# Two-layer graph attention: the third outer Strassen product by block products, a second set of sums, one order for all groups

## The chip, the cores and the metric

One core of a Trainium2 chip runs the whole kernel. The metric is the device time of one execution in microseconds, the median of several runs. TensorE (PE) multiplies and writes to PSUM banks; VectorE (DVE) and ScalarE (ACT) read and write PSUM and SBUF; GpSimd (POOL) works on SBUF; DMA transfers are issued by SyncE (SP), a few by ACT and POOL.

## The reference

128 graphs with 128 nodes and 512 features go through two attention layers with 8 heads of 64.

```
# layer 0
Q, K, V = x @ W_q + b_q, x @ W_k + b_k, x @ W_v + b_v          # by heads
scores  = Q K^T / 8 + (x @ w_g[:D])[:, None] + (x @ w_g[D:])[None, :] + b_g + log(adj + 1e-9)
x       = softmax(scores) @ V + x
# layer 1
q, k, v = x @ Wq.T + bq, x @ Wk.T + bk, x @ Wv.T + bv
logits  = q k^T / 8 + log(clip(adj, 1e-8))
out     = (softmax(logits) @ v) @ Wo.T + bo
x       = layer_norm(x + out) * gamma + beta
```

All of it is float32.

## The kernel before

**Groups.** Four graphs make a group. 32 groups (t = 0 to 31) are layer 0, the next 32 (t = 32 to 63) layer 1. A group of layer 0 has three matrices (v, q, k), each a 512 x 512 product for 4 x 128 rows; from t = 33 on each group also does the output matrix o of the group before it. Then come the scores of two graphs at a time (8 matmuls a graph, so 32 profile records for two graphs), an exponential on ACT, a product with the adjacency on DVE, and mixing with V (`mix`, 16 matmuls a graph), whose result DVE divides by the sums and writes to a tile `o`.

**Outer Strassen.** A matrix is a two-by-two product of 256 x 256 quarters with seven products P1 to P7 instead of eight. The sums of x that they need (T1 to T4, tiles `T`) are made by POOL in `outer_sums`, the sums of the weights once per weight in `combine_outer`. A product done plainly (`product`) is four units; a unit is two matmuls of 64 rows of output and 256 columns each (the two "halves", which run side by side). It takes one bank of PSUM. Each matmul is two records in the profile.

**Inner Strassen.** The products in `Strassen.INSIDE` are themselves split in 128 x 128 blocks with seven leaves (`inner`); a leaf is two half matmuls of 128 columns. Their sums come from POOL: `inner_sums` (tiles `innerB`, `innerT`) and, for weights, `combine_inner` (tile `wi`). One such product has this run in its bank: ACT fills two blocks with zero; stage 1 is two leaves; ACT copies one block to `s5` and another within the bank; stage 2 is two leaves; DVE adds `s5` to a block; stage 3 is two leaves; DVE adds again; stage 4 is one leaf. Every stage waits for the engine before it, so PE does other products, scores or mixing in between.

**A matrix.** `matrix` uses three banks: A0 or A1 by turns for P1, P6, P7 and P4, bank C for P2, bank B for P5 and, accumulated on it, P3. ACT or DVE copy partial results out (`t1`, `u2`, `u3`), and DVE adds a bank to one of these to make a quarter of the result. The first group of each layer (t = 0, 32) does all products plainly while POOL prepares the weights' inner sums. So 217 matrices of 223 have inner products: 62 groups of three, and 31 output matrices.

**Order.** Nothing is issued as it is written down. `Plan` records each operation with a cost and its predecessors, `schedule` makes list schedules with several margins, takes the best, and `refine` moves operations where PE would wait. `issue` then issues all engines' instructions in that order. Each engine runs its own in order. Every instruction therefore has one line in the profile, that of `issue` (L498); tile names tell them apart. TensorE's units have a position (`PLAIN`, `INNER_AT`, `PERIOD`) that gives a first order.

**Buffers.** `T` has one set for all groups; `innerB` and `innerT` have two each; `o` has two. The natural x of even groups of layer 0 lies in weight slot 3 (`spare`), whose weight is needed only in layer 1. In layer 1 `store_blocks` sends `o` to DRAM in four transfers for two graphs, and `load_mixed` reads it back turned.

Of the kernel before, what the change touches and what calls it, by code (L numbers as in the profile page):

```python
# [13 lines left out]
ALU = mybir.AluOpType  # L14
# [3 lines left out]
H, P, G, S = 8, 128, 4, 32  # L18
# [25 lines left out]
class Strassen:  # L44
# [6 lines left out]
    }  # L51
    SUMS = {"T1": ("B12", "B11"), "T2": ("B22", "T1"), "T3": ("B22", "B12"), "T4": ("T2", "B21")}
    RAW = {(0, 0): A11, (1, 0): A12, (1, 1): NA22, (0, 1): S3}
    INSIDE = ("P1", "P2", "P4", "P5")

    @staticmethod
    def load(engines, t, w):
# [39 lines left out]
        }  # L97


class Plan:  # L100


# [22 lines left out]

    def __init__(self, tc):
        self.tc, self.nc = tc, tc.nc
        self.ops, self.seen, self.masks, self.open, self.log = [], {}, {}, None, []
        for name in self.ENGINES:
            setattr(self, name, Plan.Engine(self, name))  # L130

    @contextmanager
    def unit(self, pos, cost):
# [25 lines left out]
    @staticmethod  # L159
    def cost(engine, method, aps, kw, args):  # L160
        n = max(a.free_size() if callable(a.free_size) else a.free_size for a in aps)
        psum = any(a.space == PSUM for a in aps)
        if method == "dma_start":
            if engine == "gpsimd":
                return 2.3, 6.5
            kb = (aps[0].size() if callable(aps[0].size) else aps[0].size) * 4 / 1024
            return 0.68 if len(aps[0].shape) == 4 else 0.47, 1.8 + kb / 150
        if engine == "scalar":
            return (0.06 + 0.00085 * n + (0.08 if "scale" in kw or "bias" in kw else 0.0) + (0.13 if "accum_out" in kw else 0.0),)
        if engine == "vector":  # L170
            if method in ("transpose", "bn_stats"):
                return (0.01 + 0.00118 * n,)
            if not psum and method in ("tensor_tensor", "tensor_scalar_mul") and n == 512:
                return (1.2,)
            return (0.08 + 0.00103 * n + (0.055 if method == "scalar_tensor_tensor" else 0.0),)
        if ALU.pow in args:
            return (0.68,)
        return (0.135 + 0.00216 * n,)
# [97 lines left out]
    def edges(self, margin, late=0.0):  # L276
        after, before = ([[] for _ in self.ops] for _ in range(2))
        for o in self.ops:
            for p in o.preds:
                wait = self.wait(self.ops[p], o) + margin * (o.engine == "tensor") + late * (self.ops[p].lag or self.CALM * (o.engine == "sync"))  # L280
                after[p].append((o.i, wait))
                before[o.i].append((p, wait))
        return after, before
# [54 lines left out]
    def refine(self, seq, before, lates):  # L338
# [123 lines left out]
        self.log.append(("refined", gained))  # L462
        return seq

    def schedule(self):
        ops, best, draw = self.ops, None, Random(1)
        _, judged = self.edges(self.JUDGED)
        lates = [
            [(0.7 * (draw.random() < 0.15), draw.expovariate(1.0) * self.ROUGH) if o.lag else (0.0, 0.0) for o in ops]
            for _ in range(self.TRIALS)  # L470
        ]
        for margin in self.MARGINS:
            after, before = self.edges(margin, self.LATE)
            key = self.first_keys(after, before)
            for n in range(self.PASSES):
                start = self.run(after, key)
                turn = sorted(ops, key=lambda o: (start[o.i], o.i))
                end = sum(self.retime(turn, judged, late) for late in lates) / self.TRIALS
                self.log.append(round(end, 1))
                if best is None or end < best[0]:  # L480
                    best = end, turn, start
                back = self.run(before, [-start[o.i] - o.cost for o in ops])
                key = [-back[o.i] - o.cost for o in ops]
                if n >= self.PASSES // 2:
                    key = [k + draw.uniform(0.0, self.STIR) for k in key]
        turn = [o.i for o in best[1]]
        for _ in range(self.SWEEPS):
            turn = self.refine(turn, judged, lates)
            self.log.append(round(sum(self.retime([ops[i] for i in turn], judged, late) for late in lates) / self.TRIALS, 1))
        self.turn = [ops[i] for i in turn]  # L490
        for o in ops:
            o.start, o.ls = best[2][o.i], 0.0
        return self.turn

    def issue(self):
# [5 lines left out]
def fast_path(ctx, tc, args, GOOD, bad):  # L501
# [8 lines left out]
    D2 = D // 2  # L510
    Q = P // S
    SCALE = 1.0 / HD**0.5
    LEAF = 0.2167
    HALVES = slice(0, P // 2), slice(P // 2, P)
    assert N == P and HD == 64 and KC == 4 and G == 4 and NG * G == B

# [31 lines left out]
    XNB = place("xn", 2, D, count=2)  # L548
    spare = W_[3][0].rearrange("p q k e -> p q (k e)")
    TB = place("T14", 2, 2, 2, N), place("T23", 2, 2, 2, N)  # L550
    TOB = [v.rearrange("p i (g c n) -> p i g c n", g=2, n=N) for v in XNB]
    INNER_B, INNER_T = Ring(place("innerB", 2, 4, N, count=2)), Ring(place("innerT", 2, 3, N, count=2))
    GW = place("gw", KC, D)
    VB = place("v", 2, 2, H, HD + 1, count=2)
    QT, KT = place("qT", 2, 4 * N, count=2), place("kT", 2, 4 * N, count=2)
    T1, U2, U3 = Ring(place("t1", 4 * N, count=2)), place("u2", 4 * N), place("u3", 4 * N)
    S5 = Ring(place("s5", N, count=4))
    HSB, OR = place("h", 2, D, count=2), Ring(place("o", 2, D, count=2))
    ROW, GAMMA, BETA, BV = place("row", D), place("gamma", D), place("beta", D), place("bv", KC)
    ZERO, ones, ident = place("zero", 2, N), place("ones", P // 2), place("ident", P)  # L560
    BQ, BK = place("bq", KC, count=2), place("bk", KC, count=2)
    bg, minus_half, good_sum, eps = place("bg", 1), place("minus_half", G), place("good_sum", 1), place("eps", 1)
    CB, GATEB, GATED = place("c", 2, G, count=2), place("gate", G, count=2), Ring(place("gated", H, count=2))
# [9 lines left out]
    def split(t):  # L573
        return t // NG, t % NG
# [57 lines left out]
    def inner_sums(xt, Bs, T):  # L632


        xs = xt[:, 0:2].rearrange("p g (k c) n -> p g k c n", k=2)
        for y, (b11, b12, b21, b22), names in (
            (INNER_B.take(), (xs[:, 0, :, 0], xs[:, 1, :, 0], xs[:, 0, :, 1], xs[:, 1, :, 1]), ("P1", "P2")),
            (INNER_T.take(), (T[:, :, 0, 0], T[:, :, 1, 0], T[:, :, 0, 1], T[:, :, 1, 1]), ("P5", "P4")),
        ):
            t1, t2, t4 = (y[:, :, j] for j in range(3))  # L640
            t3 = y[:, :, 3] if names[0] == "P1" else b12
            nc.gpsimd.tensor_tensor(t1, b12, b11, ALU.subtract)
            nc.gpsimd.tensor_tensor(t2, b22, t1, ALU.subtract)
            nc.gpsimd.tensor_tensor(t3, b22, b12, ALU.subtract)
            nc.gpsimd.tensor_tensor(t4, t2, b21, ALU.subtract)
            for k, i in enumerate(names):
                Bs[i, "inner"] = {
                    j: q[:, k] for j, q in dict(P1=b11, P2=b21, P3=b22, P4=t4, P5=t1, P6=t2, P7=t3).items()
                }


# [35 lines left out]
    def inner(i, W, Bs, bank, side, pos):  # L687
# [10 lines left out]
                    l, r = (a[j], b[j]) if side == "w" else (b[j], a[j])  # L698
                    matmul(blocks[:, at], l, r, False, True)

        nc.scalar.copy(blocks[:, C21 : 4 : 3 - C21], ZERO)
        leaves(pos[0], ("P5", 3), ("P1", C21))
        nc.scalar.copy(s5, blocks[:, 3])
        nc.scalar.copy(blocks[:, 0], blocks[:, C21])
# [4 lines left out]
        leaves(pos[3], ("P4", C21))  # L709

    PLAIN = dict(P1=10, P6=22, P7=36, P4=62, P5=38, P3=55, P2=30)
    INNER_AT = dict(P1=(0, 6, 11, 16), P4=(54, 59, 64, 69), P5=(26, 31, 43, 48), P2=(28, 33, 45, 50))
    PERIOD = 64 - 3 * len(Strassen.INSIDE)

    def matrix(n, W, Bs, side, dst, bias=None, row=None, inside=Strassen.INSIDE):
# [34 lines left out]
        add(0, 0, c, t1)  # L750
        make("P7", a, False)
        copy(u3, a, 1)
        make("P5", b, True)
        add(1, 1, b, u3)
        make("P3", b, False)
        add(0, 1, b, u2)
        make("P4", a, True)
        add(1, 0, a, u3)
# [51 lines left out]
    def score(t, graphs, pos):  # L810


        slots = [SLOTS.take() for _ in graphs]
        with nc.unit(pos, 0.92 * len(graphs) + 0.2):
            for s, b in zip(slots, graphs):
                for c in range(KC):
                    for r in range(2):
# [113 lines left out]

    tc.nc.vector.memset(ones, 1.0)
    make_identity(tc.nc, ident)
    nc.gpsimd.memset(ZERO, 0.0)
    nc.gpsimd.memset(GOOD, 0.0)
    nc.gpsimd.memset(minus_half, -0.5)
    nc.gpsimd.memset(eps, LN_EPS)
# [24 lines left out]
    n = 0  # L962
    waiting = None
    for t in range(LAST):
        L, g = split(t)
        if t == NG:
            weights(WQ, 1, 0, w_q1t)
            Strassen.combine_outer(nc.gpsimd, WQ[1][0])
            weights(WK, 1, 1, w_k1t)
            Strassen.combine_outer(nc.gpsimd, WK[1][0])  # L970
            weights(WV, 1, 3, w_v1t)
            Strassen.combine_outer(nc.gpsimd, WV[1][0])
            weights(WO, 1, 2, w_o1t)
            nc.sync.dma_start(ROW, b_o1.partition_broadcast(P))
            for c in range(KC):
                weigh_rows(c)
            Strassen.combine_outer(nc.gpsimd, WO[1][0])
# [11 lines left out]
            Strassen.combine_outer(nc.vector, WQ[0][0])  # L989
            Strassen.combine_outer(nc.vector, WK[0][0])  # L990
        TS[t] = quarters(XT[t])
        outer_sums(TS[t], TB)
        plain = t in (0, NG)
        if not plain:
            inner_sums(XT[t], TS[t], TB[0])
        if L == 0:
            gates(t)
        for which in "qkv" if t == NG else "vqk":
            if which == "v" and t != NG and t > NG + 1:
                end_attention(*waiting)  # L1000
                waiting = None
            elif which == "q" and waiting is not None:
# [13 lines left out]
        if t > NG:  # L1016
# [7 lines left out]
            if t < LAST - 1:  # L1024
                norm_and_store(u)

    t, u, a = LAST - 1, LAST - 2, n
    place_ = {"at": 0}

# [82 lines left out]
    nc.vector.tensor_scalar(bad, good, 4 * B * H * P - 0.5, None, ALU.is_lt)  # L1112
    begin_one(t, 3, HL[:, 3])
    finish_one(t, 3, HL[:, 3])
    nc.issue()


# [190 lines left out]
```

## Time and profile before

| | |
|---|---|
| median of 3 runs | 3164.75 us (3164.16 to 3164.99) |
| profiled execution, its own time | 3164.5 us |
| its span, first to last instruction | 3162.7 us |
| granted TensorE clock, mean | 0.997 |
| busy PE, PE weight loads | 3116.2, 2597.6 us |
| busy DVE, ACT, POOL | 2057.8, 1605.6, 2063.4 us |

A row of a group view reads: line, engine, operation, output<-inputs, shapes, count | busy us, mean ns of one | idle time of the engine before them, and what ended it. A row of the stretches reads: stretch, its length, then busy time with the number of instructions of PE, PE weight loads, DVE, ACT and POOL, then the granted clock, the share of the DMA engines and GB/s. A row of the instructions in order of time reads: start, length, what, how many. Matmuls are pipelined, so the length of one is longer than the step from one start to the next.

### The profile page before, as it was taken

How to read it: one execution, taken by the hardware profiler on the slowest of the kernel's cores; microseconds unless marked ns; L12 is line 12 of the kernel's file. 1: busy time of each engine (PE TensorE's matmuls, PEld its weight loads, DVE VectorE, ACT ScalarE, POOL GpSimd, SP SyncE). 2: the span in 40 equal slices, each digit the busy share in tenths (PEclk: the TensorE clock that was granted, in tenths of full speed). 3: DMA queues.
4: the chain of work that ended last, by engine and by line, in shares of the span. 5: the costliest groups of instructions: out<-in, count | busy, mean ns of one | idle time of the engine just before them, and what ended most of it. 6: DMA issues, size and time to landing. Idle time of an engine off the chain costs nothing.

```text
span 3162.7 us, 114044 instructions
## 1 busy us (share of the span) xinstructions
PE 3116.2 (99%) x47790; PEld 2597.6 (82%) x47790; DVE 2057.8 (65%) x4424; ACT 1605.6 (51%) x4528; POOL 2063.4 (65%) x2307
## 2 busy tenths in 40 slices
PE   9999999999999999999999999999999999999997
PEld 6888888888888888878888888888888888888885
DVE  5666666666666666656666666666666666666666
ACT  3555555555555545544545454544545454544543
POOL 8656666665666656696766757576766757575764
PEclk9999999999999999999999999999999999999998
DMA  5555455555555555544344443535353443535353
GB/s 128 122 119 119 103 109 123 112 109 122 110 115 105 112 120 109 127 122 102 76 111 98 104 110 90 123 85 121 85 122 84 103 110 92 122 86 121 85 110 90
DMA packets 963062, 341.43 MB, mean 108 GB/s; under 512 B 864240, under 2 KB 871408, under 8 KB 962544
## 3 DMA queue, kind: packets, MB, share of 16 engines
q1 hardware_dynamic: 944272, 299.48, 41.1%
q0 software_dynamic: 16864, 32.51, 5.9%
q8 instruction: 378, 6.19, 0.8%
q10 hardware_dynamic: 1408, 2.10, 0.2%
q14 instruction: 140, 1.15, 0.1%
HBM read 192.42 MB, written 141.56 MB: 106 GB/s over the span
## 4 chain that ended last, share of the span: by engine, by line
PE 91%; POOL 3%; ACT 2%; DVE 1%; issue 1%; DMA 0%; SPq 0%; DVEq 0%; POOLq 0%; ACTq 0%
PE bankA L498 44%; PE bankB L498 22%; PE s L498 15%; PE bankC L498 10%; ACT u L498 1%; POOL w L498 1%; POOL wi L498 1%; ACT h L498 0%; POOL T L498 0%; POOL innerB L498 0%; SPq L498 0%; DVE xT L498 0%; POOL rs L498 0%; POOL h L498 0%; POOL xn L498 0%
## 5 line engine op out<-in xcount | busy, mean ns | idle before, releaser
L498 PE MATMUL bankA<-T,w 128*64 128x256 f32 (+1 forms) x5648 | 757.4, 353 | 7.3 <-ACT u L498 5.7
L498 PEld LDWEIGHTS bankA<-T,w 128*64 128x64 f32 x5648 | 366.6, 137 | 95.5 <-ACT u L498 14.2
L498 DVE TENSOR_TENSOR bankA<-bankA,s 128x128 f32<-128x128 f32 x868 | 255.1, 294 | 282.3 <-PE bankA L498 229.9
L498 PE MATMUL bankA<-w,T 128*64 128x256 f32 (+1 forms) x2824 | 385.5, 352 | 2.4 <-POOL T L498 2.3
L498 PE MATMUL bankB<-xT,w 128*64 128x256 f32 x2048 | 306.6, 380 | 0.1
L498 ACT COPY bankB<-zero 128x256 f32<-128x256 f32 x217 | 81.6, 376 | 422.5 <-DVE kT L498 169.6
L498 DVE TENSOR_TENSOR bankB<-bankB,s 128x128 f32<-128x128 f32 x434 | 127.9, 295 | 210.4 <-PE bankB L498 183.5
L498 PEld LDWEIGHTS s<-qT,kT 64*128 64x128 f32 x4096 | 238.6, 188 | 30.0 <-issue 22.0
L498 PE MATMUL s<-qT,kT 64*128 64x128 f32 x4096 | 263.1, 278 | 0.1
L498 ACT COPY bankA<-zero 128x256 f32<-128x256 f32 x434 | 164.4, 379 | 192.1 <-DVE u L498 108.0
L498 POOL TENSOR_TENSOR xn<-gw 128x512 f32<-128x512 f32 x62 | 79.1, 1276 | 258.7 <-DVE gw L498 81.5
L498 POOL TENSOR_TENSOR T<-xT 128x512 f32<-128x512 f32 x128 | 162.2, 1287 | 118.5 <-PE bankB L498 59.6
L498 ACT COPY s<-bankA 128x128 f32<-128x128 f32 x434 | 116.5, 268 | 232.1 <-PE bankA L498 225.8
L498 PEld LDWEIGHTS bankA<-w,T 128*64 128x64 f32 x2824 | 182.4, 137 | 36.0 <-POOL T L498 4.1
L498 DVE SCALAR_TENSOR_TENSOR h<-adjT,s 128x1024 f32<-128x1024 f32 x128 | 154.7, 1215 | 68.9 <-ACT s L498 68.3
L498 ACT ACTIVATE gw<-gw 128x512 f32<-128x512 f32 x256 | 163.0, 640 | 52.6 <-POOL gw L498 51.1
L498 POOL TENSOR_TENSOR gw<-w,gw 128x512 f32<-128x512 f32 x128 | 161.9, 1286 | 41.4 <-ACT gw L498 41.4
L498 POOL TENSOR_TENSOR gw<-xn,gw 128x512 f32<-128x512 f32 x128 | 161.6, 1283 | 37.2 <-ACT gw L498 37.1
L498 DVE TENSOR_TENSOR bankC<-bankC,s 128x128 f32<-128x128 f32 x434 | 126.7, 292 | 90.4 <-PE bankC L498 66.0
L498 PE MATMUL bankA<-w,xn 128*64 128x256 f32 x1364 | 183.6, 352 | 0.0
L498 DVE STREAM_TRANSPOSE xT<-xT 128x512 f32<-128x512 f32 x252 | 172.9, 695 | 12.4 <-DMA xT<-in_x_dram 10.4
L498 DVE SCALAR_TENSOR_TENSOR xT<-adjT,s 128x1024 f32<-128x1024 f32 x124 | 148.8, 1215 | 46.4 <-ACT s L498 41.5
(218 smaller groups left out, 8827.0 us busy)
## 6 DMA issues: line engine op xcount, KB each, us to landing
xT<-x1d_b SPq DMA_DIRECT2D x64, 512.0 KB, 6.4
xT<-in_x_dram SPq DMA_DIRECT2D x496, 64.0 KB, 2.9
x1d_o<-o SPq DMA_DIRECT2D x248, 128.0 KB, 4.5
gw<-x1d_o SPq DMA_DIRECT2D x62, 512.0 KB, 3.5
h<-x1d_n POOLq DMA_DIRECT2D x62, 512.0 KB, 9.7
out_dram<-h SPq DMA_DIRECT2D x60, 512.0 KB, 2.9
xn<-in_x_dram SPq DMA_DIRECT2D x32, 512.0 KB, 4.5
x1d_n<-w SPq DMA_DIRECT2D x32, 512.0 KB, 3.0
```

Of the source, the lines that this page charges most:

```text
L498: self.tc.keep_in_program_order(getattr(getattr(self.nc, engine), method)(*args, **kw))
```

## The change

P3 becomes an inner product: it gets its own turn in bank B or C by turns, and DVE adds that bank to `u2` before `u2` is added to P5's bank. POOL makes three more block sums (`inner3`, two buffers) and one in place; the `innerB` sum that had a fourth column is now also made in place. `wi` has room for five products, and `combine_inner` makes the sums of five. The zero fill no longer copies a tile of zeros: ACT multiplies the identity matrix, read twice, by zero. `o` has one buffer. Even groups of layer 0 put their outer sums into idle parts of slot 3 (`TB0`). In layer 1 the v weights are loaded and combined first, and group 32 does v, q, k like the others. `schedule` orders the operations of groups 1 to 31 and of 34 to 62 by one written list of keys per layer (`PATTERNS`), repeated for each group, before `refine` runs; some of the planner's costs are changed.

```diff
-    INSIDE = ("P1", "P2", "P4", "P5")
+    INSIDE = ("P1", "P2", "P3", "P4", "P5")
...
+PATTERNS = (
+    (1, 31, 42.01, [int(v) for v in '''
+        413 877 68 1327 2833 345 136 0 481 1462 1395 1039 549 2070 3356 809 626 694 1573 2772 8615 4503 9355 9402
...
+    (34, 62, 52.97, [int(v) for v in '''
...
+    def periodic(self, start):
+
+        ops, marks, key, shift = self.ops, self.marks, list(start), 0.0
+        for first, last, period, at in self.patterns:
...
+            for t in range(first, last + 1):
+                for r, x in enumerate(at):
+                    key[marks[t] + r] = origin + period * (t - first) + x / 100
...
+        heap, seq = [], []
+        for o in ops:
+            if not left[o.i]:
+                heappush(heap, (key[o.i], o.i))
+        while heap:
+            i = heappop(heap)[1]
+            seq.append(i)
+            for j in after[i]:
+                left[j] -= 1
+                if not left[j]:
+                    heappush(heap, (key[j], j))
+        return seq
...
-        turn = [o.i for o in best[1]]
+        turn = self.periodic(best[2])
...
+    TB0 = [
+        v.rearrange("p (i g c) n -> p i g c n", i=2, g=2)
+        for v in (W_[3][0][:, 4:6].rearrange("p q k (c n) -> p (q k c) n", n=N), W_[3][1].rearrange("p i j n -> p (i j) n")[:, 0:8])
+    ]
...
-    INNER_B, INNER_T = Ring(place("innerB", 2, 4, N, count=2)), Ring(place("innerT", 2, 3, N, count=2))
+    INNER_B, INNER_T, INNER_3 = (
+        Ring(place(name, n, 3, N, count=2)) for name, n in (("innerB", 2), ("innerT", 2), ("inner3", 1))
+    )
...
-    HSB, OR = place("h", 2, D, count=2), Ring(place("o", 2, D, count=2))
+    HSB, OR = place("h", 2, D, count=2), Ring(place("o", 2, D, count=1))
...
+            (INNER_3.take(), (ys[:, 0, 1:, 0], ys[:, 1, 1:, 0], ys[:, 0, 1:, 1], ys[:, 1, 1:, 1]), ("P3",)),
         ):
             t1, t2, t4 = (y[:, :, j] for j in range(3))
-            t3 = y[:, :, 3] if names[0] == "P1" else b12
             nc.gpsimd.tensor_tensor(t1, b12, b11, ALU.subtract)
             nc.gpsimd.tensor_tensor(t2, b22, t1, ALU.subtract)
-            nc.gpsimd.tensor_tensor(t3, b22, b12, ALU.subtract)
+            nc.gpsimd.tensor_tensor(b12, b22, b12, ALU.subtract)
             nc.gpsimd.tensor_tensor(t4, t2, b21, ALU.subtract)
...
-        nc.scalar.copy(blocks[:, C21 : 4 : 3 - C21], ZERO)
+        nc.scalar.mul(blocks[:, C21 : 4 : 3 - C21], ident.rearrange("p (o n) -> p o n", o=1).to_broadcast([P, 2, N]), 0.0)
...
-    INNER_AT = dict(P1=(0, 6, 11, 16), P4=(54, 59, 64, 69), P5=(26, 31, 43, 48), P2=(28, 33, 45, 50))
+    INNER_AT = dict(P1=(0, 6, 11, 16), P3=(9, 14, 19, 24), P4=(54, 59, 64, 69), P5=(30, 35, 43, 48), P2=(3, 8, 13, 18))
...
+        if "P3" in inside:
+            d = (b, c)[n % 2]
+            make("P3", d, True)
+            nc.vector.tensor_tensor(u2, d, u2, ALU.add)
         make("P5", b, True)
         add(1, 1, b, u3)
-        make("P3", b, False)
+        if "P3" not in inside:
+            make("P3", b, False)
         add(0, 1, b, u2)
...
         if t == NG:
+            weights(WV, 1, 3, w_v1t)
+            Strassen.combine_outer(nc.gpsimd, WV[1][0])
             weights(WQ, 1, 0, w_q1t)
...
-        outer_sums(TS[t], TB)
+        sums = TB if L or t % 2 else TB0
+        outer_sums(TS[t], sums)
...
-        for which in "qkv" if t == NG else "vqk":
+        for which in "vqk":
```

## The prediction

> **What bounds the kernel now.** I read the page first, then the stretches between the first score matmuls of chosen groups, then single TensorE instructions in order of time, then the rows by shape, then what TensorE waited for.
>
> ```profile
> span 3162.7 us, 114044 instructions
> PE 3116.2 (99%) x47790; PEld 2597.6 (82%) x47790; DVE 2057.8 (65%) x4424; ACT 1605.6 (51%) x4528; POOL 2063.4 (65%) x2307
> ...
> PE 91%; POOL 3%; ACT 2%; DVE 1%; issue 1%; DMA 0%; SPq 0%; DVEq 0%; POOLq 0%; ACTq 0%
> ```
>
> TensorE (PE) is the bound: 99% busy and 91% of the chain that ended last. The next view cuts the span at the first score matmul of groups 1, 31, 34 and 62 (columns as its header says):
>
> ```profile
> 0.00:101.10 101.10, 92.31 (x1116) 69.17 (x1116) 58.31 (x102) 38.99 (x108) 82.05 (x120) 0.98 0.59 131
> 101.10:1378.70 1277.60, 1273.38 (x20148) 1081.41 (x20146) 835.25 (x1800) 712.11 (x2066) 804.19 (x818) 1.00 0.55 116
> 1378.70:1526.70 148.00, 144.24 (x2072) 115.43 (x2070) 88.59 (x178) 58.95 (x154) 114.27 (x164) 1.00 0.35 81
> 1526.70:3055.50 1528.80, 1519.11 (x23284) 1265.24 (x23282) 1009.07 (x2211) 757.63 (x2101) 1008.00 (x1146) 1.00 0.44 103
> ```
>
> 30 middle groups of layer 0 take 1277.60/30 = 42.59 us each, 28 of layer 1 take 1528.80/28 = 54.60. The clock is full. Per group DVE has 27.8 us and POOL 26.8 in layer 0; 36.0 and 36.0 in layer 1. What PE needs without any stall comes from the steps between starts:
>
> ```profile
> 843.64 0.60 PE L498 MATMUL bankA<-T,w 128*64 128x256 f32 x4
> 844.07 0.39 PE L498 MATMUL bankA<-innerB,wi 128*64 128x128 f32 x4
> 844.29 0.39 PE L498 MATMUL bankA<-xT,w 128*64 128x128 f32 x4
> 844.50 0.60 PE L498 MATMUL bankA<-T,w 128*64 128x256 f32 x4
> ...
> 1435.20 1.99 PE s L498 x32
> 1442.10 0.93 PE s L498 x32
> ```
>
> A plain unit (256 columns, both halves) steps 0.432 us, a leaf (128 columns) 0.218 as the trace's usual value, the scores of two graphs 1.99, one graph's mixing 0.93. A product by leaves is 7 x 0.218 = 1.526, a plain one 4 x 0.432 = 1.728. A matrix now is 4 x 1.526 + 3 x 1.728 = 11.29. So a layer-0 group needs 3 x 11.29 + 2 x 1.99 + 4 x 0.93 = 41.6 and a layer-1 group, with four matrices, 52.9. Measured 42.59 and 54.60: stalls of 1.0 and 1.7 us a group, 78 us in these 58 groups.
>
> **A rule weighed here.** PE's row shows only 1277.60 - 1273.38 = 4.2 us idle in layer 0 and 9.7 in layer 1. The Trainium skill, "Trainium Kernel Development and Optimization", section Performance Expectations, says that matmul busy time is a bad metric because matmuls are pipelined, and to take LDWEIGHTS busy instead. By PE's row a new order could save 14 us in the middle at most; by the LDWEIGHTS row (82%) some 560 in all; by the steps 78. The trace's steps decide: the rule is right about the busy row, but its substitute is far off here.
>
> ```profile
> PE bankA L498 <- ACT bankA L498: 6.0, 16, 0.9
> PE bankA L498 <- ACT u L498: 5.7, 5, 3.8
> PE bankA L498 <- POOL T L498: 2.3, 2, 1.6
> ```
>
> The waits that the trace names are few and mostly for a bank's zero fill or copies (ACT); sums from POOL cost PE two waits in the whole run.
>
> **Part 1: P3 by seven block products.** 217 of the 223 matrices (31 + 31 groups of three, 31 output matrices) change. *PE:* out go 4 plain units, in come 7 leaves: 1.728 - 1.526 = 0.20 us a matrix, 217 x 0.20 = **-43.4 us**, on the path because PE is the path. *A rule against it:* "TensorEngine Tiling (Array Packing)", Performance Considerations, Instruction Overhead: "Each matmul has ~60 cycle overhead on TRN2". The change issues 14 matmuls for 8, 1302 more; 60 cycles of the 2.4 GHz that "TensorE: Matmul & The Clock Gate" gives in its head table are 25 ns, an estimate of 33 us, which would leave 11 us of gain. The row says otherwise: two leaves step 0.436, one plain unit 0.432, so a split costs 2 ns a matmul, and that is already in 0.218. I take the row.
>
> *DVE:* two adds inside the bank and one into u2. The rows by shape:
>
> ```profile
> L498 DVE TENSOR_TENSOR bankB<-bankB,s 128x128 f32<-128x128 f32 x434 | 127.9, 295 | 210.4 <-PE bankB L498 183.5 <-ACT bankA L498 11.4 <-ACT bankC L498 4.3
> L498 DVE TENSOR_TENSOR v<-bankB,u 128x512 f32<-128x512 f32 x128 | 88.0, 688 | 61.1 <-PE bankB L498 54.3 <-ACT s L498 4.5 <-ACT u L498 2.0
> L498 ACT COPY bankB<-zero 128x256 f32<-128x256 f32 x217 | 81.6, 376 | 422.5 <-DVE kT L498 169.6 <-DVE v L498 118.9 <-DVE qT L498 70.2
> L498 ACT COPY s<-bankB 128x128 f32<-128x128 f32 x217 | 57.6, 266 | 63.9 <-PE bankB L498 60.3 <-PE bankC L498 0.6
> L498 ACT COPY bankB<-bankB 128x128 f32<-128x128 f32 x217 | 54.8, 252 | 3.1
> ```
>
> 2 x 0.295 + 0.688 = 1.28 us a matrix: layer 0 27.8 + 3.8 = 31.7 of about 42 us (75%), layer 1 36.0 + 5.1 = 41.1 of about 53.5 (77%). *ACT:* 0.376 + 0.266 + 0.252 = 0.89 a matrix: 23.7 to 26.4 and 27.1 to 30.6, under 65%. *POOL:* four 128x128 sums per set; that shape takes 0.45 us in the weights' sums, so 1.8: layer 0 26.8 to 28.6, layer 1 (two sets) 36.0 to 39.6. All beside PE's work, so costed at nothing; the cover is a quarter of DVE idle. If it is gone, the slow rival below follows.
>
> *All 1085 fills* become an activation of the identity matrix times zero. The trace has no such form. Nearest is the copy of the same shape from SBUF (0.38); above it stands the 128x256 activation with a bias from a bank (0.475); nothing excludes 0.05 less than the copy. I take 0.38. At 0.475 it would hurt only fills whose first leaf follows the bank's last PE use by 1.4 us or less: about 144 of them, 14 us; at the low end it gives 7 back.
>
> *Weights:* combine_inner does five more sums per weight matrix, 35 x 0.45 us on POOL: 15 at the start, 20 at the layer change. There POOL runs almost without a break (114.27 of 148.00 us; 82.05 of the first 101.10) and PE stalls about 12 us at the start and 9 at the change. POOL's queue delays the first sums of the next groups. Bounds: 0, and all of it exposed, 6.8 + 9.0. I take +2 and **+4**.
>
> **Part 2: second set of outer sums in layer 0.** Even groups write their sums into idle space of weight slot 3. POOL waited 107 us in layer 0 before T<-xT for PE to finish with the old sums; that idle time goes. TensorE waited for POOL's T only in three weight loads of that stretch, 1.1 us in all, so I cost it at **0** (at most 1 us of gain); the hiding work is PE's own, and it buys slack for POOL's extra 1.8 us. Layer 1's first weights for slot 3 have to wait for group 30's sums, but the same slot held that group's natural x before, so no later. The first layer-1 matrix becomes v instead of q; its weights have their combination first in POOL's order. No gain counted.
>
> **One buffer for o instead of two.** In layer 1 the second pair's DVE write of o now waits for the first pair's store: four SP issues (2.99 us at 2025.28) and 4.5 us of landing, about 8 us after the last write. In the changed order the first pair's last mixing and the second pair's first stand 8.7 us of PE work apart. I take 0; if it is late by 1 us in each group, DVE's whole queue stands behind it, the stage adds too, up to 28 us. SP's and POOL's numbers of DMA issues stay.
>
> **Part 3: one order.** The changed program has only two PE orders per layer, for even and odd groups; now all middle groups differ. The fixed numbers in the patterns are keys; I take no time from them. Stage distances by PE work decide what it costs. In the trace of before, set against its own order, a first leaf within 1.4 us of the bank's last PE use stalls about 0.12 us, within 1.1 us 0.18; a third stage 0.4 us behind the second 0.11; a fourth 0.2 behind the third 0.34; larger distances almost nothing. The new layer-0 group has on average two first leaves at 1.3 and one third stage at 0.44: 0.35 us. The new layer-1 group has a fourth stage at 0.22, two first leaves at 1.3 and one at 1.09: 0.76. Scores (0.2), plain products' hand-offs (0.3) and small waits in leaves (0.15) are left as they are: 1.0 and 1.4 us, against 1.0 and 1.7 now. So layer 0 gives 0 and layer 1 28 x 0.3 = 8; as irregular groups (52.3 to 57.3 us now) become alike, I add 2: **-10**.
>
> **Sum:** -43.4 - 10 + 4 + 2 = -47.4; the profiled execution took 3164.5 (span 3162.7 and 1.8 around it), so 3117. The median 3164.75 lies 0.25 higher, which changes nothing. After it a layer-0 group should take about 42.0 us, a layer-1 group 53.5.
>
> **Rivals.** *The order is worth more than its product* (0.18). All groups become as good as today's best: 41.1 - 0.6 is too much to hope, but stalls of 0.6 in both layers give 12 + 31 us below today, with 43 of work and 6 lost at the edges: 3084, and 3100 if half of it comes. For it: the spread among today's groups. Against: tight stages repeat in every group.
>
> *The gain is half eaten* (0.12). Before's stall rates carried over to every distance of the whole new order give 131 us instead of 110: +21, and the edges' 6: 3164.5 - 43.4 + 27 = 3148; 10 more if all of POOL's edge work is exposed.
>
> *DVE's queue sets the pace* (0.07, slower). Each new 0.688 add into u2 can stand before a stage add whose leaf is due. From 0.20 us of extra PE stall a matrix the gain is gone; at half an add, 0.34, it is 217 x 0.14 = 30 us slower: 3195. For it: DVE at 77%, distances of 0.87 us between stages as the rule, banks B and C with three turns per two matrices more evenly full. Against: today's stages at that distance stall 0 to 11 ns, with DVE at 66%.
>
> **Numbers.** The main case has 0.60, and 0.03 goes to no change: within 0.2% (6.3 us, about what a measurement of this kernel tells from none). Faster 0.89 (0.60, 0.18 and most of the half-eaten case), slower 0.08 (DVE, and that case with o's wait on top). The range 3090 to 3148 leaves out the slow rival, no change, and the far ends of the other two; all unknown costs but the full 28 us of o lie within it.
>
> **What would show it.** PE matmul records up by 2604; PE time in the middle groups 42.0 and 53.5 us; weight loads busier than 82%; DVE near 75%, POOL near 72%, fills near 380 ns; DVE not waiting for the store of o. It is wrong if a layer-1 group stays above 54.2 (stages wait for DVE or o), or if the change of layers takes over 10 us more than 148.

## The result and the profile after

The changed kernel takes 3134.5 us (median of 4 runs, 3132.6 to 3136.7) against 3164.5 before: ratio 0.9906, 95% interval 0.9889 to 0.9923. The prediction was 3117, range 3090 to 3148. The direction was right and the time lies in the range, but 30 of the forecast 47 us came.

The page of the kernel after, its span, busy times and chain by engine:

```profile
span 3133.3 us, 121185 instructions
PE 3079.3 (98%) x50394; PEld 2667.8 (85%) x50394; DVE 2262.5 (72%) x5075; ACT 1796.7 (57%) x5179; POOL 2233.0 (71%) x2713
...
PE 88%; POOL 4%; DVE 2%; ACT 2%; issue 2%; DMA 1%; SPq 0%; ACTq 0%; DVEq 0%; POOLq 0%
```

The stretches between the first score matmuls of groups 1, 31, 34 and 62, as they were shown of before (stretch, its length, busy PE, PE weight loads, DVE, ACT, POOL, clock, DMA share, GB/s):

```profile
0.00:102.90 102.90, 94.14 (x1170) 71.69 (x1170) 61.28 (x112) 39.13 (x110) 85.99 (x138) 0.97 0.52 110
102.90:1376.10 1273.20, 1266.37 (x21164) 1096.75 (x21162) 906.81 (x2063) 787.98 (x2331) 842.55 (x933) 1.00 0.55 117
1376.10:1535.40 159.30, 147.12 (x2129) 117.75 (x2128) 96.57 (x198) 66.95 (x179) 125.56 (x187) 0.98 0.37 85
1535.40:3021.50 1486.10, 1480.53 (x24650) 1310.24 (x24650) 1125.60 (x2548) 859.14 (x2438) 1114.60 (x1379) 1.00 0.45 107
3021.50:3133.30 111.80, 91.11 (x1292) 71.33 (x1290) 72.26 (x156) 43.48 (x123) 64.25 (x80) 0.93 0.37 91
```

| stretch | before, us | after, us | stalls before | stalls after |
|---|---|---|---|---|
| start | 101.1 | 102.9 | 12.3 | 13.8 |
| 30 groups of layer 0, each | 42.59 | 42.44 | 31.5 in all | 51.0 |
| change of layers | 148.0 | 159.3 | 8.4 | 21.0 |
| 28 groups of layer 1, each | 54.60 | 53.07 | 51.0 | 29.7 |
| tail | 107.2 | 111.8 | 6.6 | 8.7 |

A stall here is the step from one matmul's start to the next less the usual step for that pair of shapes in the trace of before. All of them together grew by 14.4 us, from 109.8 to 124.2; the span fell by 29.4. The difference, 43.8 us, is PE's shorter work: P3's whole saving was made, and a third of it was given back. Layer 1's stretch gained 42.7 us and layer 0's 4.4, and the start, the change and the tail lost 17.7. Stretch and stalls together show PE's work, and not all of it stays on its side of a cut: in layer 0's stretch the work fell by 4.4 + 19.5 = 23.9 us, where P3's 90 products save 18; the other 6 us moved across the cuts into other stretches (the tail's work grew by 4.6 - 2.1 = 2.5). So layer 0 by itself gained nothing: its stalls took all that P3 saves there.

**Layer 0.** Its groups do not all take 42.44: by turns they take 42.9 (from an even group's first score to the next) and 42.1. Rows chosen from the instructions in order of time show the largest difference between the two, first in an even group, then in an odd one:

```profile
573.25 1.09 ACT L585 ACTIVATE s<-s,c 128x1024 f32<-128x1024 f32 x1
573.84 0.30 DVE L585 TENSOR_TENSOR bankA<-bankA,s 128x128 f32<-128x128 f32 x1
574.27 0.39 PE L585 MATMUL bankC<-w,xT 128*64 128x128 f32 x4
574.37 1.22 DVE L585 SCALAR_TENSOR_TENSOR h<-adjT,s 128x1024 f32<-128x1024 f32 x1 [0.23 <-ACT s L585]
575.50 0.29 DVE L585 TENSOR_TENSOR bankC<-bankC,s 128x128 f32<-128x128 f32 x1
575.94 0.44 PE L585 MATMUL bankC<-w,inner 128*64 128x128 f32 x4 [0.21 <-DVE bankC L585]
```

```profile
616.87 0.30 DVE L585 TENSOR_TENSOR bankA<-bankA,s 128x128 f32<-128x128 f32 x1
617.09 1.22 DVE L585 SCALAR_TENSOR_TENSOR h<-adjT,s 128x1024 f32<-128x1024 f32 x1
617.30 0.39 PE L585 MATMUL bankB<-w,xT 128*64 128x128 f32 x4
618.23 0.29 DVE L585 TENSOR_TENSOR bankB<-bankB,s 128x128 f32<-128x128 f32 x1
618.67 0.44 PE L585 MATMUL bankB<-w,inner 128*64 128x128 f32 x4
```

P3's stage 3 (bank C in the even group) is on PE at 574.27, but its add stands on DVE behind the adjacency product, 1.22 us long, which itself waited 0.23 us for ACT's exponential. The last leaf starts at 575.94; on average over the even groups PE stalls 0.38 us there. In odd groups P3 is in bank B, and the adjacency product starts at 617.09, before the stage-3 leaf at 617.30; the stall is 0.08. The trace's list of PE's waits in this stretch (what waits, for what, us in all, how many, longest) has bank C and DVE's add first; 14 of the 15 are this place, in the even groups 2 to 28:

```profile
PE bankC L585 <- DVE bankC L585: 3.2, 15, 0.2
```

Three first leaves in banks C and B cost even groups 0.4 us more, ACT's fill being late. So what the distance rates of before could not show is what DVE has in front of an add: a place costs by its neighbours in DVE's queue. The even groups' extra 0.8 us make some 12 of the 19.5 us by which layer 0's stalls grew; the rest, in odd groups too, was not traced.

**The change of layers.** Chosen rows of the instructions in order of time, one engine after the other. ACT:

```profile
1380.92 0.63 ACT L585 ACTIVATE gw<-gw 128x512 f32<-128x512 f32 x1 [3.20 <-POOL gw L585]
1381.68 1.09 ACT L585 ACTIVATE s<-s,c 128x1024 f32<-128x1024 f32 x1
```

DVE and PE:

```profile
1382.80 1.22 DVE L585 SCALAR_TENSOR_TENSOR h<-adjT,s 128x1024 f32<-128x1024 f32 x1 [3.72 <-ACT s L585]
...
1384.07 2.00 PE L585 MATMUL s<-v,h 128*64 128x65 f32 x32 [4.50 <-DVE h L585]
...
1388.08 2.00 PE L585 MATMUL s<-v,h 128*64 128x65 f32 x32 [2.01 <-DVE h L585]
```

POOL:

```profile
1379.62 1.27 POOL L585 TENSOR_TENSOR gw<-xn,gw 128x512 f32<-128x512 f32 x1
1380.84 1.27 POOL L585 TENSOR_TENSOR T<-xT,T 128x512 f32<-128x512 f32 x1
1382.06 1.27 POOL L585 TENSOR_TENSOR w<-w 128x512 f32<-128x512 f32 x1
...
1383.77 1.28 POOL L585 TENSOR_TENSOR gw<-xn,gw 128x512 f32<-128x512 f32 x1
```

Between two of group 31's gate sums (gw) POOL makes an outer sum of group 32 (T) and a step of layer 1's weight sums (w), so the next gate sum starts only 4.15 us after the last. ACT, in order, waits for a gate sum with the exponential of the scores behind it; DVE's adjacency product waits for that, and PE's mixing for it: 4.50 and 2.01 us. After the longer pause the clock is halved: the stretch 1384.1 to 1390.9 has a granted clock of 0.50, and each mixing lasts 2.00 us instead of 0.93. Before, the granted clock of the whole change was 1.00.

**The start.** SP's queue in the kernel after issues five of group 1's turned x (xT), 3.46 us in all, ahead of its part of group 0's x (w, as that x lies in weight slot 3):

```profile
0.74 3.46 SPq L585 DMA_DIRECT2D xT<-in_x_dram  x5
4.76 1.09 SPq L585 DMA_DIRECT2D w<-in_x_dram  x2
```

PE then waits 4.0 us for that x (w<-in_x_dram), and the clock is 0.50 from 8.5 to 15.3 us; before, its first wait for a transfer was 1.9 us, and the clock was full up to 24 us.

### The profile page after: what moved, and what is told of

Same layout as the page of the kernel before. It is cut to its first block, busy times and chain, and to the rows that moved or that the text cites. A ratio compares the mean times of both kernels' runs of the same rounds, so it can differ in the third digit from the quotient of the medians.

```text
span 3133.3 us, 121185 instructions
## 1 busy us (share of the span) xinstructions
PE 3079.3 (98%) x50394; PEld 2667.8 (85%) x50394; DVE 2262.5 (72%) x5075; ACT 1796.7 (57%) x5179; POOL 2233.0 (71%) x2713
## 4 chain that ended last, share of the span: by engine, by line
PE 88%; POOL 4%; DVE 2%; ACT 2%; issue 2%; DMA 1%; SPq 0%; ACTq 0%; DVEq 0%; POOLq 0%
PE bankA L585 42%; PE bankB L585 16%; PE bankC L585 15%; PE s L585 15%; POOL gw L585 2%; ACT s L585 1%; DVE kT L585 1%; POOL w L585 1%; ACT gw L585 1%; DMA xT<-in_x_dram 1%; POOL T L585 1%; POOL wi L585 0%; SPq L585 0%; DVE bankB L585 0%; POOL inner L585 0%
## 5 line engine op out<-in xcount | busy, mean ns | idle before, releaser
L585 PE MATMUL bankA<-T,w 128*64 128x256 f32 (+1 forms) x4232 | 519.8, 351 | 1.1 <-ACT bankA L585 0.8
L585 DVE TENSOR_TENSOR bankB<-bankB,s 128x128 f32<-128x128 f32 x650 | 193.0, 297 | 214.3 <-PE bankB L585 170.8
L585 PEld LDWEIGHTS bankA<-T,w 128*64 128x64 f32 x4232 | 276.3, 137 | 46.3 <-ACT bankA L585 1.0
L585 DVE TENSOR_TENSOR bankC<-bankC,s 128x128 f32<-128x128 f32 x652 | 192.4, 295 | 156.5 <-PE bankC L585 125.7
L585 ACT ACTIVATE bankA<-ident 128x256 f32<-128x256 f32 x434 | 167.5, 386 | 197.4 <-DVE kT L585 117.9
L585 PE MATMUL bankA<-w,T 128*64 128x256 f32 (+1 forms) x2116 | 271.2, 352 | 0.9 <-POOL w L585 0.9
L585 PE MATMUL bankC<-xT,w 128*64 128x128 f32 (+1 forms) x2296 | 228.2, 277 | 0.4 <-ACT bankC L585 0.4
L585 POOL TENSOR_TENSOR h<-h,gamma 128x512 f32<-128x512 f32 x121 | 154.7, 1280 | 36.7 <-ACT h L585 36.7
L585 ACT ACTIVATE bankC<-ident 128x256 f32<-128x256 f32 x326 | 126.7, 389 | 91.3 <-DVE kT L585 48.6
L585 ACT ACTIVATE bankB<-ident 128x256 f32<-128x256 f32 x325 | 124.3, 383 | 87.6 <-DVE qT L585 34.8
```

Of the source, the lines that this page charges most:

```text
L585: self.tc.keep_in_program_order(getattr(getattr(self.nc, engine), method)(*args, **kw))
```

## The experiments

Stretches are named as above. "Written order" is the list of keys per layer.

**Without the written order**

```diff
-    nc.patterns = PATTERNS
+    nc.patterns = ()
```

> The changed kernel with the written order taken away (the planner orders all groups as before). Theory: the written order is what lowered layer 1's stalls from 1.7 to 1.0 us a group, and P3's extra turn alone raises stalls; so without it layer-1 groups at 54.2 to 54.8 us, layer-0 groups at 42.3 to 42.8, the run at 3155 to 3170. Rival (the order is worth nothing, P3's shorter PE work is the whole gain): layer 1 stays at 53.1, the run at 3130 to 3140.

3164.3 us, ratio to before 0.9996 (0.9987 to 1.0005). Layer-1 groups 54.77 (1533.7 / 28), layer-0 groups 42.43, start 95.9, change 151.5. Stalls in layer 1 are 78.4 us against 29.7. All of it lies where the theory had it. So the change without its written order is no gain over the kernel before. For the new operations the written order is worth 1.7 us a group in layer 1, 48 us, and nothing in layer 0's middle.

**Also with P3 plain**

```diff
-    INSIDE = ("P1", "P2", "P3", "P4", "P5")
+    INSIDE = ("P1", "P2", "P4", "P5")
...
-            (INNER_3.take(), (ys[:, 0, 1:, 0], ys[:, 1, 1:, 0], ys[:, 0, 1:, 1], ys[:, 1, 1:, 1]), ("P3",)),
...
-    nc.patterns = PATTERNS
+    nc.patterns = ()
```

> The changed kernel without the written order and with P3 plain on P5's bank; the second set of sums, one buffer for o, the fill from the identity and v first at the change of layers stay. Theory: these other edits are worth nothing in the middle groups, 42.6 and 54.6 us as in the kernel before, and lose a few us at the change of layers if v first is to blame: 3160 to 3175. Rival (the second set of sums is what matters): layer-0 groups at 42.2 or less, 3150. Against the run without the written order, P3 alone is then worth between +43 us (all of its PE work kept) and nothing (all of it given back in stalls).

3176.7 us, ratio 1.0033 (1.0021 to 1.0046). Layer-1 groups 55.03, layer-0 groups 42.04. My theory missed: layer-0 groups are at the rival's number without the rival's total, and the run is 1.7 us above my range. Against the run above, P3's block products save 0.26 us of their 0.8 in a layer-1 group (no more than another draw of the planner moves, see below) and cost 0.39 in a layer-0 group, a loss of 4 over the middles; the 12 us between the two runs come from the edges (start 101.1 against 95.9, change 158.2 against 151.5, and the tail). Against the kernel before, the other edits, among them the planner's changed costs and stage positions, lose 12 us: layer 0's middle is 16 shorter, the change of layers 10, layer 1's middle 12 and the tail 6 longer.

**Written order in layer 1 only**

```diff
-    nc.patterns = PATTERNS
+    nc.patterns = PATTERNS[1:]
```

> The changed kernel with the written order in layer 1 only. Theory: layer 1 keeps 53.1 us a group; layer 0's 0.65 us of extra stall comes from DVE and ACT being fuller and P3's turn in bank C of even groups, so the planner's own order does no better: 42.3 to 42.8, the run at 3128 to 3145. Rival (the written order itself is what costs layer 0): layer-0 groups at 42.0, the run at 3115 to 3122. If the change of layers also shrinks from 159 us towards 148, it was the pattern's end that delayed it.

3118.0 us, ratio 0.9850 (0.9833 to 0.9866), 16.5 faster than the changed kernel. Layer 1 is the same; so are layer 0's groups on average. The gain is at both ends of layer 0:

```profile
0.00:95.40 95.40, 88.07 (x1120) 68.37 (x1120) 63.10 (x109) 40.02 (x112) 88.19 (x137) 1.00 0.58 128
95.40:1368.40 1273.00, 1264.90 (x21210) 1106.30 (x21208) 918.93 (x2066) 788.02 (x2340) 849.02 (x943) 1.00 0.56 118
1368.40:1517.90 149.50, 143.88 (x2130) 115.37 (x2128) 94.97 (x196) 63.77 (x170) 116.80 (x178) 1.00 0.33 76
1517.90:3004.10 1486.20, 1480.67 (x24648) 1309.97 (x24648) 1124.78 (x2548) 859.08 (x2437) 1114.24 (x1379) 1.00 0.45 107
```

Start 95.4 and change 149.5, both with a clock of 1.00. In SP's queue group 0's x is first again:

```profile
0.75 0.86 SPq L585 DMA_DIRECT2D w<-in_x_dram  x2
```

My expectation that layer 0's middle would be no better was right, but the total fell below its range, to the rival's number: I had looked for the written order's cost in the middle, and it was at the ends.

**q, k, v and their weights first, as before, at the change of layers**

```diff
-            weights(WV, 1, 3, w_v1t)
-            Strassen.combine_outer(nc.gpsimd, WV[1][0])
             weights(WQ, 1, 0, w_q1t)
...
+            weights(WV, 1, 3, w_v1t)
+            Strassen.combine_outer(nc.gpsimd, WV[1][0])
...
-        for which in "vqk":
+        for which in "qkv" if t == NG else "vqk":
```

> The changed kernel with q, k, v order in group 32 and the q and k weights first, as before. Theory: the 12 us lost at the change of layers come from POOL's weight sums standing in front of the gate sums of group 31, which delays ACT's exponential, DVE's adjacency product and PE's mixing; who is first among v, q, k does not matter: stretch 155 to 162 us, the run at 3130 to 3138. Rival (v first is to blame): stretch 148 to 151, the run at 3124.

3139.1 us, ratio 0.9911 (0.9894 to 0.9928); the change of layers takes 158.7 us, as the theory said, and the total is 1 us above its range. Which matrix comes first is not what costs there.

**Layer 0's written order for groups 2 to 29 only**

```diff
-    (1, 31, 42.01, [int(v) for v in '''
+    (2, 29, 42.01, [int(v) for v in '''
```

> The changed kernel with layer 0's written order for groups 2 to 29 instead of 1 to 31. Theory: the written order costs layer 0 only at its ends: it puts group 1's loads in front of group 0's in SP's queue, and POOL's weight sums in front of group 31's gate sums; in between it is as good as the planner's (42.5). So the start falls from 102.9 to 95 to 98 us and the change of layers from 159 to 148 to 152: 3115 to 3125. Rival (the start and the change lose time to P3's extra sums of the weights on POOL, not to the order's ends): 3131 to 3137.

3125.9 us, ratio 0.9875 (0.9860 to 0.9891), 1 us above the range of the theory, which holds for both ends: start 95.2, change 151.3. The run with the written order in layer 1 only gains 17 us at the two ends (7.5 and 9.8); with the order's ends alone taken away, 15.7 of them come back, though P3's extra weight sums on POOL are all still there. The middle, with new seams at groups 2 and 30, loses 6.7 (1279.9).

**P3's banks exchanged, written order kept**

```diff
-            d = (b, c)[n % 2]
+            d = (c, b)[n % 2]
```

> The changed kernel with banks B and C exchanged for P3, the written order kept. Theory: even groups of layer 0 take 42.9 us and odd ones 42.1 because the bank that P3 takes by turns is kept by P2 or P5 at a time that the order meets badly in even groups; exchanged, odd groups become the slow ones or both change by more than 0.3 us. Rival (even groups are slow because of their own buffers, the sums and x in weight slot 3): even 42.9, odd 42.1 as now.

One run, 3482.5 us. In layer 0 the odd groups are now the ones with 42.9 and the even ones have 42.1: it is the bank that P3 takes, not the even groups' buffers, that makes every second group slow. In layer 1 each group takes 64.9 us:

```profile
1551.60:3368.80 1817.20, 1619.40 (x24642) 1294.29 (x24642) 1130.66 (x2548) 855.50 (x2442) 1111.55 (x1376) 1.00 0.37 87
```

My theory did not foresee that. PE's longest waits in the whole run are for the fills (ACT) and stage adds (DVE) of the two banks:

```profile
PE bankB L585 <- ACT bankB L585: 57.0, 92, 1.6
PE bankC L585 <- DVE bankC L585: 51.7, 127, 0.7
PE bankB L585 <- DVE bankB L585: 48.7, 114, 0.8
```

A written order fits one assignment of banks. With the other one PE works 57.8 of 64.9 us by its row, with the same instructions.

**Second set of sums in the kernel before**

```diff
-        outer_sums(TS[t], TB)
+        sums = TB if L or t % 2 else TB0
+        outer_sums(TS[t], sums)
```

> The kernel before with the second set of outer sums for even groups of layer 0, and nothing else. Theory: the second set frees the planner of the order between groups in layer 0 and is worth about 0.5 us a group: layer-0 groups at 42.0 to 42.2 instead of 42.58, layer 1 and the edges as before, 3147 to 3155. Rival (the prediction's: POOL's waits for these tiles lie beside PE's work): 3161 to 3166, layer-0 groups at 42.5 or more.

3184.2 us, ratio 1.0063 (1.0047 to 1.0078), layer-0 groups 42.97. My theory, formed on the 42.04 of the run with P3 plain, fell; and the prediction's rival did not hold to its range either. With fewer constraints the planner made another order, and a worse one; whether the second set or chance did that, one run does not tell.

**The planner's draw from 2, kernel before**

```diff
-        ops, best, draw = self.ops, None, Random(1)
+        ops, best, draw = self.ops, None, Random(2)
```

> The kernel before with the planner's draw of random numbers started from 2 instead of 1, nothing else. Theory: the planner's orders for the same operations differ by chance by as much as the second set of sums moved the kernel before (+18.5 us): 3150 to 3190, layer-0 groups off 42.58 by 0.2 or more, layer-1 groups off 54.60 by 0.2 or more. Rival (the draw hardly matters, and the second set itself harms): 3160 to 3169.

3171.9 us, ratio 1.0020 (1.0011 to 1.0028): layer-0 groups 42.45, layer-1 groups 54.88, start 106.9, change 144.7. My theory held for the total and layer 1, not for layer 0, which moved by 0.13. So the same operations move by 6 us from one draw to another, by up to 0.3 us a group and 6 us at the start. Differences of that size between two planned orders say nothing about the edit; the 18.5 of the second set are more, but one pair does not show how far a draw can go.

**One set of sums, written order in layer 1 only**

```diff
-    nc.patterns = PATTERNS
+    nc.patterns = PATTERNS[1:]
...
-        sums = TB if L or t % 2 else TB0
+        sums = TB
```

> Written order in layer 1 only, P3 by block products in both layers, one set of outer sums in layer 0. Theory: the second set is worth little by itself; against the same kernel with two sets (3118.0, layer-0 groups 42.42) layer-0 groups move by chance within 0.4 us. Rival (with P3 in layer 0 the second set is needed for POOL's extra work): layer-0 groups at 43 or more, 3135 or more.

3165.2 us, ratio 0.9999 (0.9990 to 1.0008): 47 us slower than with two sets. My theory fell, and the rival's numbers came: layer-0 groups take 43.89. Layer 0's stretch:

```profile
97.90:1414.70 1316.80, 1283.33 (x21237) 1108.01 (x21234) 920.69 (x2070) 790.15 (x2337) 853.20 (x944) 1.00 0.53 113
```

The longest wait of its POOL in that stretch:

```profile
POOL T L585 <- PE bankA L585: 199.8, 33, 13.0
```

POOL waits 199.8 us for PE to finish with the old sums; with two sets this wait is not among POOL's rows in layer 0. PE itself never waits long for T: it waits more for DVE's adjacency product (s<-h: 5.6 us in 16 waits, with two sets none in its list). That POOL's lateness reaches PE by way of ACT and DVE, as at the change of layers, fits this but was not followed step by step. With P3 by block products in layer 0 the second set is worth 1.5 us a group. That is five times what a draw moved a group.

**P3 by block products in layer 1 only, written order in layer 1 only**

```diff
+    FOUR = ("P1", "P2", "P4", "P5")
...
-            inner_sums(XT[t], TS[t], sums[0])
+            inner_sums(XT[t], TS[t], sums[0], Strassen.INSIDE if L else Strassen.FOUR)
...
-    nc.patterns = PATTERNS
+    nc.patterns = PATTERNS[1:]
```

(and the same choice in the matrices and in the weights' inner sums)

> The changed kernel with the written order in layer 1 only and P3 by block products in layer 1 only; layer 0 has P3 plain on P5's bank and the planner's own order. Theory: in layer 0 P3's block products give all of their PE work back in stalls (42.42 us a group with them, 42.04 to 42.19 without, both with the second set of sums), so this is faster than the written order in layer 1 alone (3118) by 6 to 11 us: 3107 to 3112, layer-0 groups at 42.0 to 42.2, layer-1 groups at 53.1. Rival (the planner's order differs by chance between the two runs by as much): 3115 to 3122.

3112.4 us, ratio 0.9832 (0.9819 to 0.9846), the fastest of all, at the upper end of my range, and 22 us faster than the changed kernel:

```profile
0.00:101.20 101.20, 92.81 (x1144) 71.03 (x1144) 62.12 (x107) 39.56 (x110) 86.19 (x125) 1.00 0.60 138
101.20:1363.70 1262.50, 1261.33 (x20070) 1073.68 (x20068) 819.43 (x1789) 724.21 (x2062) 795.04 (x812) 1.00 0.55 117
1363.70:1512.20 148.50, 143.62 (x2128) 115.82 (x2128) 96.37 (x198) 63.12 (x170) 116.96 (x181) 1.00 0.34 81
1512.20:2998.60 1486.40, 1480.80 (x24648) 1309.85 (x24648) 1125.98 (x2548) 860.09 (x2438) 1115.63 (x1379) 1.00 0.45 107
```

Layer-0 groups take 42.08 us, 0.35 less than with the shorter PE work (42.43), and DVE has 3.3 us less to do in each. Stalls in layer 0 are 22.5 us against 47.3 in the run with the written order in layer 1 only.

**P3 in layer 1 only, and the written order in layer 1 only, each again with the planner's draw from 2**

> Written order in layer 1 only, P3 by block products in layer 1 only, the planner's draw from 2. Theory: layer-1 groups stay at 53.1 (the written order does not depend on the draw), layer 0 and the edges move by chance; layer-0 groups 41.9 to 42.4: 3100 to 3130. Rival (P3 plain is better in layer 0 only by the first draw): layer-0 groups at 42.5 or more.

3113.5 us, ratio 0.9837 (0.9820 to 0.9853), layer-0 groups 42.11, layer-1 groups 53.14.

> Written order in layer 1 only, P3 by block products in both layers, the planner's draw from 2. Theory: layer 0's stalls eat P3's PE work again, groups at 42.3 to 42.9, 0.2 to 0.5 us above those with P3 plain and the same draw: 3110 to 3135. Rival (P3 is worth its 0.6 us in layer 0 and the first draw was bad luck): layer-0 groups at 41.6 to 42.0.

3123.8 us, ratio 0.9868 (0.9851 to 0.9884), layer-0 groups 42.48, layer-1 groups 53.15. Same picture with another draw: in layer 0 P3's block products cost 0.37 us a group more than they save. Both layer-1 numbers stay, since that order does not come from the draw.

## Why the prediction was right or wrong

The total lies in the range partly by luck. Of the forecast by stretch, layer 1 came 10 us better, layer 0 14 us worse and the start, the change and the tail together 15 us worse; the time stands midway between the main case, 3117, and the rival with the gain half eaten, 3148, and neither describes it.

**PE's work, -43.4: right.** 2604 more matmul records, and 43.8 us less work by the sum of spans and stalls. The step of 0.218 for a leaf carried over, so the sixty-cycle rule that spoke against the change indeed does not apply to these matmuls. PE's busy row was no measure, as the prediction took it: it had 9.7 us idle in layer 1, where stalls then fell by 21.3. (The section on it that the prediction names puts MFU beside the LDWEIGHTS row; the prediction weighed only the row.)

**DVE, ACT and POOL beside PE, nothing: half right.** Their loads came out near the forecast: ACT 57%, POOL 71%; DVE 72% instead of 75%, as rows that follow each other at once overlap (in layer 0's stretch DVE's rows add up to 1020 us and cover 907). In layer 1 their extra work is hidden; in layer 0 it is not, though DVE is there at 71% (906.81 of 1273.20), less than layer 1's 76%. The slow rival came near the mechanism, a stage add behind a longer DVE instruction. But it named the new add into u2 where the trace has the adjacency product, which was there before, and took it for a matter of DVE's load; it is a matter of place in the queue.

**The written order, 0 in layer 0 and -10 in layer 1: wrong in size, both ways.** Layer 1's stalls fell by 21.3 us, twice the forecast, and layer 0's rose by 19.5. The step that failed is the table of stalls by distance. It said 0.76 us for the four tight places of a layer-1 group; three of them, the first leaves, cost nothing (all 560 first leaves stall 0.2 us together), and only the fourth stage at 0.22 us cost what it said (0.35): it is the one large stall of a layer-1 group. In layer 0 it gave 0.35 a group and left out the fourth stage of P3, which lies at a distance that cost nothing before. Rates from one order, where an engine's queue is what it happens to be, don't carry to another.

**What the order is worth, missed.** The prediction gave P3's product 43 us and the order 10. The runs show that they cannot be priced apart: without the written order P3 and the rest give nothing (0.9996), and with it layer 1 is 48 us faster. These 48 us are stalls, 78.4 down to 29.7: with the planner's order the new stages stalled more than before's 51.0 and ate most of P3's shorter work, with the written one less. Of layer 1's 42.7 us against the kernel before, about half is P3's shorter work and half fewer stalls. A written order for layer 1 with P3 plain was not run: the list has one key for each operation of a group and does not fit another set of operations. The prediction also asked of the even split of turns over banks B and C only how full they are; the exchanged banks show how much hangs on which is used when.

**Second set of sums, 0: wrong.** I costed it at nothing since PE hardly waited for POOL's T (for all of POOL's results five waits, 3.1 us, in the run before, where the prediction counted two). That was a reading of an order made for one set. With P3's extra work in layer 0 it is worth 47 us (the run with one set of sums). In the kernel before it was no gain.

**Start +2 and change +4: too small.** +1.8 and +11.3. The second is over the 10 us that the prediction itself had set as a sign of being wrong. The change's step named POOL's extra weight sums; the run with the written order for groups 2 to 29 keeps them and gives the loss back. Its cause is the place of gate sums among the weight sums and T's, which the written order sets at its end. The start's +1.8 is right by accident: the planner's start with P3 is 3 to 6 us faster than before's (95.4 to 97.9 us in the four runs with P3 by block products and no written order in layer 0), and the written order puts five transfers in front of the first x on SP's queue, which the prediction did not look at. It said only that the number of transfers stays.

**Fills and o: right.** The fill from the identity takes 383 to 389 ns against 376 to 379. DVE never waited for the store of o: its idle time before o is 0.5 us in the whole trace, and none of it for a transfer.

**Still open.** Why the edits other than P3 lose 10 us at the change of layers without P3's block products and 3 with them, where both have the planner's own order; and whether some order of layer 0 makes P3's block products pay there. Layer-0 groups with P3 plain take 42.04 to 42.11 us in three runs of the changed program and 42.58 in the kernel before: the second set alone does not bring this (42.97), and the changed planner costs and stage positions were not tried alone. The tail takes 110.3 to 113.3 us in the runs of the changed program and 107.2 to 107.6 in those of the kernel before, with P3 by block products or without; no run says which edit does it. Two buffers for o, and the copy from a zero tile, were not tried either.

## What to carry to other kernels

A saving on the bound engine is worth its size only in an order that can use it: check where the new stages stand in the other engines' queues, above all behind which long instruction, and not only how busy these engines are. A wait that is free in one order need not be in another, so an edit that loosens an order is judged together with the work that is added, not by the old trace alone. And where a planner or search makes the order, run it with another draw first: what that moves is the least that a comparison of two edits has to show.

## What the runs showed that I had not expected

Two short pauses of PE, 4.5 and 2.0 us (at the change of layers), cost more than themselves: the clock went to 0.50 for 6.8 us, and two mixings took 2.00 us each instead of 0.93. The pause of 4.0 us at the start was followed by another 6.8 us at 0.50. The Trainium skill, "TensorE: Matmul & The Clock Gate", Part 1, has such a halving after one idle window of 3.4 us; here the half clock lasted twice that long, and the run with the written order in layer 1 only has a clock of 1.00 both there and at the start.

An order that repeats exactly gives times that repeat exactly: layer-1 groups of the kernel after take 53.0 to 53.2 us nearly throughout, where they took 52.3 to 57.3. And the same instructions with two banks exchanged take 64.9.
